# Expert weights carried in the exchanged rows, the gates' exponential by a power on GpSimd, and another order of drain and first loads: a gated cross-attention and mixture-of-experts block in float32 on one core

## The chip, the cores and the metric

The kernel runs on one core of a Trainium2 chip; the other cores are idle. The time is the device time of one execution in microseconds (us), and lower is better. All data and all arithmetic are float32 (indices are int32). Five engines work from queues of their own, each strictly in the order in which its instructions were written: TensorE (PE, with its weight loads PEld), VectorE (DVE), ScalarE (ACT), GpSimd (POOL) and SyncE (SP, which here only issues DMA transfers). They wait for one another by semaphores.

## The reference, cut to what matters

32 sequences of 128 tokens with 128 features, so 4096 tokens; 16 attention heads of 8 features; 8 routed experts (each token uses the best two) and 2 shared experts, all with 512 hidden units.

```python
x = x + tanh(g_xattn) * attention(layernorm(x), ctx, ctx, mask)      # 16 heads, softmax over 128 keys
xf = layernorm(x)
shared = mean over 2 experts of  gelu(xf @ sW1 + sb1) @ sW2 + sb2
gates = xf @ rW + rb                                                 # 8 gates per token
topk_vals, topk_idx = top_k(gates, 2)
topk_probs = softmax(topk_vals)
w = sum(topk_probs[..., None] * onehot(topk_idx))                    # two nonzero weights per token
h = gelu(xf @ W1[e] + b1[e]);  y[e] = h @ W2[e] + b2[e]
moe = sum over e of w[:, e] * y[e]
out = x + tanh(g_ffn) * (shared + moe)
```

## The kernel before, in words

**Stages.** The 32 sequences form 8 blocks of 4 (`BB`). A hand-written software pipeline runs over 32 steps (one sequence each) and 4 more that drain it; a step is two half-steps, numbered `where` = 0 to 7 within a block, and in each half-step `chores` inserts pieces of other work at the places `part` = -1, 0, 1, 2. These pieces are Python generators that are advanced one `yield` at a time: `before` (the next block's projections), `normed`, `after` (a finished block's second normalisation, gates, top two, and the slots of its rows), `sent` (the rows' scatter), and the filler `shared` (the two shared experts for a block). Since each queue runs in the order written, these insertions are the schedule.

**The filler.** `shared(i)` gives 8 pieces "h" (one matmul of 128x512 into a PSUM tile `ph`, L657, and its gelu on ACT, L661), then for each of 4 sequences a piece "y" (8 matmuls into `py`, L669) and a piece "a" (DVE adds `py` to the result rows `acc`, L676). `fill(kind)` advances it by one piece if the next one is of that kind, `more(n)` by n pieces. `ph`, `py`, and the small PSUM tiles `pu`, `pt_f`, `pgt`, `pr` share two PSUM buffers ("misc"), so each new one waits until the last but one has been read. The hidden values `h` have one buffer in the pool `ffn`.

**Gating and exchange.** `after` (L525 on) scales the rows into `xf[0]` on POOL (L315, L317), transposes them (`pt_f`) and multiplies by the gate weights (`pgt`, L548). DVE finds the best two by comparing all pairs (L554 to L579); POOL copies and advances the running counts (`front`, `seen`, L583 and L584). A step of its own (L587 to L601) takes exp on ACT and leaves both weights of each token, times tanh(g_ffn), in `wk2`. The next step ranks the rows by two small matmuls (`pr`, L604 and L607) and gives the slots `to_i` (L622). A row has 132 numbers (`ROW`): 128 features, the row's destination as an integer in column 128, and three unused columns. `sent` copies a sequence's rows to `xf[1]` and scatters both copies with an indirect DMA each (L634) to the DRAM buffer `xs`, which is sorted by expert.

**Schedule of the tiles.** After the last block `schedule` computes on DVE, from the counts (`pn`, L701), which expert and rows each of 39 tiles (32 of 256 rows, 7 of 128) gets: `ps_i` (L707), `table` (L756, L782), and the tiles' first-layer biases `b1t` (L786 to L795, 15 operations). Its scratch tile `space` lies in the pool `blk`. Then the attention's pools are closed, the pool `rt` is opened in their space, and the rest of filler blocks 4 and 5 is written ahead of the routed tiles. On SP, `padded` writes padding rows (L802) and `routed` loads, for each tile, two weight matrices (L814, L815), a bias row spread over the partitions (`b2t`, L818) and the rows (`xt`, L830). The first five tiles' weights are all issued ahead of their rows (L834, L835); afterwards the loads run five tiles ahead.

**Routed tiles.** Per tile PE transposes the rows (`pt_r`), does the first layer (`phr`, L855, gelu on ACT) and, one tile later, the second (`pyr`, L869). DVE adds `b2t` (L874), and POOL scatters each half of the result to its destination in the DRAM buffer `yd` (L879). Buffers: six for the weights and `b2t`, seven for `xt`, four for `y`.

**Tail.** After the last tile SP fetches `yd` by blocks (`y2`, L911), while PE does the filler of blocks 6 and 7. `combine` adds, for each of 4 sequences and 2 choices, `wk2` times the row (L920, eight operations of 128x128 a block), and `store` writes the rows out (L926).

Of the kernel before, what the change touches and what calls it, by code (L numbers as in the profile page):

```python
# [15 lines left out]
P = 128  # L16
BB = 4
# [16 lines left out]
def flamingo_kernel(  # L34
# [151 lines left out]
    nc.gpsimd.memset(mhalf, -0.5)  # L186
    ones = const.tile([P, P], F32, name="ones")
# [106 lines left out]
    wk2 = wts.tile([P, n_blocks * BB, 2], F32, name="wk2")  # L294
# [229 lines left out]
    def after(i, st):  # L524
# [55 lines left out]

        front = small.tile([P, BB, E], F32, tag="front", name=f"front_{i}")
        for b in range(BB):
            nc.gpsimd.tensor_copy(front[:, b, :], seen)  # L583
            nc.gpsimd.tensor_tensor(seen, seen, both[:, b, :], ALU.add)  # L584
        yield

        nc.scalar.activation(ge, ge, AF.Exp)  # L587
        gk = small.tile([P, 2, BB, E], F32, tag="gk", name=f"gk_{i}", bufs=1)
        nc.vector.tensor_tensor(
            gk, hot, ge.unsqueeze(1).to_broadcast([P, 2, BB, E]), ALU.mult  # L590
        )
        wk = small.tile([P, 2, BB], F32, tag="wk", name=f"wk_{i}")
        nc.vector.tensor_reduce(wk, gk, AX.X, ALU.add)
        ws = small.tile([P, BB], F32, tag="ws", name=f"ws_{i}")
        nc.vector.tensor_tensor(ws, wk[:, 0], wk[:, 1], ALU.add)
        nc.vector.reciprocal(ws, ws)
        nc.vector.tensor_scalar(ws, ws, tg[:, 1:2], None, ALU.mult)
        for k in range(2):
            nc.vector.tensor_tensor(
                wk2[:, i * BB : (i + 1) * BB, k], wk[:, k], ws, ALU.mult  # L600
            )  # L601
# [21 lines left out]
        st.update(xf=xf, to_i=to_i)  # L623
        yield
# [23 lines left out]


    def shared(i, two):  # L650
        h = ffn.tile([P, NS * NC, NB], F32, tag="h", name=f"h_{i}", bufs=1)
        for u in range(NS * NC // 2):
            ph2 = two(f"ph_{i}_{u}")
            for n in range(2):
                k, c = divmod(2 * u + n, NC)
                ph = ph2[n]
                nc.tensor.matmul(  # L657
                    ph, lhsT=W1_sb[:, k, c * P : (c + 1) * P], rhs=xfT_all[:, i, :],
                    start=True, stop=True,
                )  # L660
                nc.scalar.activation(  # L661
                    h[:, k * NC + c, :], ph, AF.Gelu,
                    bias=sb1c[:, k * NC + c : k * NC + c + 1],
                )
                yield "h"
        for b in range(BB):
            py = misc(f"py_{i}_{b}")[:, :P]
            for kc in range(NS * NC):
                nc.tensor.matmul(  # L669
                    py, lhsT=h[:, kc, b * P : (b + 1) * P],  # L670
                    rhs=W2_sb[:, kc // NC, kc % NC, :],
                    start=(kc == 0), stop=(kc == NS * NC - 1),
                )
            yield "y"
            a = acc[:, i * BB + b, :]
            nc.vector.tensor_tensor(a, py, a, ALU.add)  # L676
            yield "a"


    def schedule(ps_i, table, b1t):  # L680

        space = blk.tile([P, 2, BB, 2, P], F32, tag="kh", name="space").rearrange(
            "p s b j k -> p (s b j k)"
        )
        used = 0

        def temp(shape):
            nonlocal used
            size = math.prod(shape[1:])
            o = space[:, used : used + size]  # L690
            used += size
# [93 lines left out]
        part = temp([P, n_tiles, NC])  # L785
        for e in range(E):  # L786
            o = b1t if e == 0 else part
            nc.vector.tensor_tensor(
                o, mine[:, :, e : e + 1].to_broadcast([P, n_tiles, NC]),
                b1c[:, e, :].unsqueeze(1).to_broadcast([P, n_tiles, NC]), ALU.mult,  # L790
            )
            if e:
                nc.vector.tensor_tensor(b1t, b1t, part, ALU.add)
            if e % 3 == 2:
                yield  # L795
# [40 lines left out]
    def routed(table, b1t):  # L836
        weights = [load_weights(t, table) for t in order[:DEEP]]
        loaded = {t: (*w, load_rows(t, table)) for t, w in zip(order, weights)}

# [23 lines left out]
        def second(t, h):  # L863
# [3 lines left out]
            for n in range(parts(t)):  # L867
# [7 lines left out]
                y[:, : parts(t)], py, b2t.unsqueeze(1).to_broadcast([P, parts(t), P]), ALU.add  # L875
            )
# [39 lines left out]
    def combine(i, y2):  # L916
        for b in range(BB):
            for k in range(2):
                a = acc[:, i * BB + b, :]
                nc.vector.scalar_tensor_tensor(  # L920
                    a, y2[:, k, b, :], wk2[:, i * BB + b, k : k + 1], a, ALU.mult, ALU.add
                )
# [48 lines left out]
    with tc.manual_schedule(  # L971
# [12 lines left out]
        def chores(i, b, odd, part):  # L984
# [12 lines left out]
            elif part == 1:  # L997
                if where == 2:
                    step(behind)
                    fill("h") or fills("y")  # L1000
                elif where in (0, 6):
                    fills("y")
# [34 lines left out]
            elif where == 6:  # L1037
# [3 lines left out]
                step(behind)  # L1041
# [9 lines left out]
        def drain(where, part):  # L1051
# [3 lines left out]
            if part == 1:  # L1055
                if where > 2:
                    more(1)
                return
            if where == 0:
                step(behind)  # L1060
                ready.append(n_blocks - 2)
                step(sending)
                fills("y", "a")
            elif where == 1:
                step(behind)
                step(behind)
                step(sending)
                fills("y", "a")
# [5 lines left out]
            elif where == 3:  # L1074
                step(behind)
# [67 lines left out]
        more(2)  # L1143
        step(sending)
        for n in (3, 0, 3, 2, 1, 2):
            step(behind)
            more(n)
        sending = sent(last)
        ready.append(n_blocks - 1)
# [3 lines left out]
        steps = schedule(ps_i, table, b1t)  # L1153
        while step(steps):
# [5 lines left out]
        rt = ctx.enter_context(tc.tile_pool(name="rt", bufs=2))  # L1160
# [66 lines left out]
```

## Time and profile before

| what | value |
|---|---|
| median of 3 runs | 569.68 us (567.11 to 570.94) |
| the profiled execution | 571.77 us, of which the span of its instructions is 570.0 us |
| mean granted TensorE clock | 0.958 |
| DVE, ACT, POOL busy | 52%, 47%, 49% of the span |
| DMA moved | 53.82 MB, mean 94 GB/s |

The page of a profile lists busy time by engine, slices of the span with the TensorE clock that was granted (1.00 is full speed), the chain of work that ended last, and groups of instructions with what ended the idle time before them. Stretches of the span can be asked for one by one. By the start of their first instruction the stages are: preparation to about 20 us, the attention pipeline to 297 us, its drain with the last gating and the tile schedule to about 394 us, the routed tiles to 533 us, and the tail.

### The profile page before, as it was taken

What the parts mean: (1) busy time and instruction counts of PE and PEld (TensorE: products, weight loads), DVE (VectorE), ACT (ScalarE), POOL (GpSimd) and SP (SyncE); (2) the same over time, 40 slices, a digit from 0 to 9 for tenths busy, and PEclk for the clock granted to TensorE, in tenths of its full rate; (3) what the DMA queues carried; (4) which work ended last, traced back from release to release, by engine and by line L of the source; (5) the groups of instructions that cost most, each with busy time, mean ns of one, the idle gap of its engine ahead of it and who ended that gap; (6) DMA issues with size and microseconds to landing.
All of it is one profiled execution on the core that took longest, in us unless ns stands there. A gap on an engine that the chain in (4) does not pass through costs nothing.

```text
span 570.0 us, 11053 instructions
## 1 busy us (share of the span) xinstructions
PE 499.4 (88%) x3740; PEld 347.2 (61%) x3740; DVE 298.3 (52%) x961; ACT 266.8 (47%) x483; POOL 280.5 (49%) x559
## 2 busy tenths in 40 slices
PE   0586999989899898998989799788999999999977
PEld 0243545455565554546655377457999998888655
DVE  5445777596866877768782223821122221222186
ACT  1232757657644477565443533422445444444512
POOL 9541316158476585763836734600456455445400
PEclk9967999989999999999995799979999999999999
DMA  6410201002012010000000100365578788787293
GB/s 189 146 55 1 56 2 57 1 1 80 15 34 63 2 37 20 11 31 1 25 16 16 38 16 11 115 153 156 154 205 238 228 242 230 222 233 203 71 295 106
DMA packets 67719, 53.82 MB, mean 94 GB/s; under 512 B 6104, under 2 KB 59184, under 8 KB 67664
## 3 DMA queue, kind: packets, MB, share of 16 engines
q1 hardware_dynamic: 62016, 42.59, 27.3%
q0 software_dynamic: 5072, 10.26, 5.3%
q8 instruction: 30, 0.49, 0.3%
q10 hardware_dynamic: 576, 0.26, 0.2%
q14 instruction: 25, 0.20, 0.1%
HBM read 39.84 MB, written 13.25 MB: 93 GB/s over the span
## 4 chain that ended last, share of the span: by engine, by line
PE 62%; DVE 19%; DMA 6%; POOL 4%; ACT 3%; issue 3%; SPq 3%; POOLq 0%; DVEq 0%; ACTq 0%
PE pyr L869 10%; PE phr L855 9%; PE sc L414 8%; PE ph L657 7%; PE py L669 6%; DVE mexp L431 6%; PE num L472 4%; PE pk L374 3%; DMA xt<-xs 2%; PE pu L487 2%; DMA b2t<-in_L_ffn_b_dram 2%; DVE kT L377 2%; PE sw L414 2%; PE pq L358 2%; PE pgt L548 1%
## 5 line engine op out<-in xcount | busy, mean ns | idle before, releaser
L879 POOL DMA_INDIRECT yd<-y,xt x71 | 67.9, 957 | 94.3 <-DVE y L874 48.8
L431 DVE TENSOR_REDUCE mexp<-sc 128x4 f32<-128x512 f32 x128 | 82.2, 685 | 40.8 <-PE sw L414 34.2
L858 ACT ACTIVATE hr<-phr,b1t 128x256 f32<-128x256 f32 (+1 forms) x156 | 64.5, 454 | 79.1 <-PE phr L855 70.5
L464 ACT ACTIVATE pT<-sw 128x1024 f32<-128x1024 f32 x64 | 65.7, 1026 | 65.6 <-PE sw L414 65.6
L414 PE MATMUL sc<-kh,qT 32*128 32x256 f32 x512 | 77.4, 416 | 10.3 <-DVE mexp L431 10.1
L414 PE MATMUL sw<-qm,kT 32*128 32x256 f32 x512 | 76.7, 417 | 0.0
L657 PE MATMUL ph<-xfT_all,W_sb 128*128 128x512 f32 x128 | 67.1, 644 | 6.6 <-ACT h L661 2.4
L634 POOL DMA_INDIRECT xs<-xf,to_i x64 | 64.2, 1003 | 16.6 <-issue 6.7
L661 ACT ACTIVATE h<-ph,cols 128x512 f32<-128x512 f32 x64 | 43.9, 687 | 60.6 <-PE ph L657 60.4
L414 PEld LDWEIGHTS sc<-kh,qT 32*128 32x128 f32 x512 | 48.7, 192 | 35.8 <-issue 20.2
L869 PE MATMUL pyr<-w,hr 128*128 128x128 f32 x568 | 69.6, 275 | 0.0
L855 PE MATMUL phr<-xT,w 128*128 128x256 f32 (+1 forms) x312 | 68.1, 361 | 1.6 <-DVE xT L846 1.1
L669 PE MATMUL py<-W_sb,h 128*128 128x128 f32 x512 | 63.0, 283 | 6.0 <-DVE acc L676 6.0
L669 PEld LDWEIGHTS py<-W_sb,h 128*128 128x128 f32 x512 | 61.3, 199 | 10.4 <-DVE acc L676 6.3
L869 PEld LDWEIGHTS pyr<-w,hr 128*128 128x128 f32 x568 | 66.4, 192 | 0.5
L855 PEld LDWEIGHTS phr<-xT,w 128*128 128x128 f32 x312 | 53.0, 191 | 7.0 <-DVE xT L846 1.3
L381 POOL TENSOR_SCALAR kh<-kT,half 128x512 f32<-128x512 f32 x32 | 22.4, 714 | 61.3 <-DVE kT L377 61.3
L414 PEld LDWEIGHTS sw<-qm,kT 32*128 32x128 f32 x512 | 46.9, 192 | 0.9 <-issue 0.4
L846 DVE COPY xT<-pt_r 128x256 f32<-128x256 f32 (+1 forms) x39 | 15.6, 401 | 59.3 <-PE pt_r L844 58.8
L472 PE MATMUL num<-pT,v 128*32 128x256 f32 x512 | 42.9, 408 | 2.1 <-DVE qm L450 2.1
L657 PEld LDWEIGHTS ph<-xfT_all,W_sb 128*128 128x128 f32 x128 | 21.0, 198 | 35.3 <-ACT h L661 20.2
L874 DVE TENSOR_TENSOR y<-pyr,b2t 128x256 f32<-128x256 f32 (+1 forms) x39 | 15.6, 401 | 48.7 <-PE pyr L869 45.9
(210 smaller groups left out, 713.9 us busy)
## 6 DMA issues: line engine op xcount, KB each, us to landing
w<-in_L_ffn_W_dram SPq DMA_DIRECT2D x78, 256.0 KB, 3.2
xt<-xs SPq DMA_DIRECT2D x32, 132.0 KB, 4.1
y<-yd SPq DMA_DIRECT2D x16, 256.0 KB, 5.3
b2t<-in_L_ffn_b_dram SPq DMA_DIRECT2D x39, 64.0 KB, 8.3
x<-in_x_dram SPq DMA_DIRECT2D x8, 256.0 KB, 2.6
c<-in_ctx_dram SPq DMA_DIRECT2D x8, 256.0 KB, 4.2
mf<-md SPq DMA_DIRECT2D x7, 256.0 KB, 4.9
out_dram<-acc SPq DMA_DIRECT2D x7, 256.0 KB, 4.1
```

What stands on the lines that cost most here:

```text
L414: nc.tensor.matmul(out[:, r, s * 256 : s * 256 + 256], lhsT=lhsT[rr, s, :], rhs=rhs[rr, s, :, :].rearrange("p j n -> p (j n)"), start=True ...
L431: nc.vector.tensor_reduce(m[:, r], a["sc"][:, r, :].rearrange("p (s j k) -> p s j k", s=2, j=2), AX.X, ALU.max,)
L464: nc.scalar.activation(a["pT"][:, 2 * n : 2 * n + 2, :], a["sw"], AF.Exp)
L472: nc.tensor.matmul(num[32 * r : 32 * r + 32, :], lhsT=v[:, b, r, s, :], rhs=a["pT"][:, r, s * 256 : s * 256 + 256], start=True, stop=True,)
L634: ins = nc.gpsimd.indirect_dma_start(out=xs[:, :], out_offset=bass.IndirectOffsetOnAxis(ap=to_i[:, k, b : b + 1], axis=0), in_=xf[k][:, b, :],
L657: nc.tensor.matmul(ph, lhsT=W1_sb[:, k, c * P : (c + 1) * P], rhs=xfT_all[:, i, :], start=True, stop=True,)
L661: nc.scalar.activation(h[:, k * NC + c, :], ph, AF.Gelu, bias=sb1c[:, k * NC + c : k * NC + c + 1],)
L669: nc.tensor.matmul(py, lhsT=h[:, kc, b * P : (b + 1) * P], rhs=W2_sb[:, kc // NC, kc % NC, :], start=(kc == 0), stop=(kc == NS * NC - 1),)
L855: nc.tensor.matmul(ph, lhsT=w1[:, c * P : (c + 1) * P], rhs=xT, start=True, stop=True)
L858: nc.scalar.activation(h[:, c, :size], ph, AF.Gelu, bias=b1t[:, t, c : c + 1])
L869: nc.tensor.matmul(py[:, n, :], lhsT=h[:, c, n * P : (n + 1) * P], rhs=w2[:, c, :], start=(c == 0), stop=(c == NC - 1),)
L879: ins = nc.gpsimd.indirect_dma_start(out=yd[:, :], out_offset=bass.IndirectOffsetOnAxis(ap=xt.bitcast(I32)[:, n, P : P + 1], axis=0), in_= ...
```

## The change

Rows carry their weight: column 129 of `xf[k]` receives the weight of choice k, so the scatter brings it to the tile and the tile multiplies its result by it; `wk2` is gone and `combine` becomes two additions of 128x512 a block. The weights come from one number e2 = e^(second best gate - best gate): POOL computes it as a power of a constant, and DVE makes w0 = tanh(g_ffn) / (1 + e2) and w1 = w0 * e2 in the last step of `after`, behind `to_i`. The step with exp on ACT is gone, so `after` has one step fewer.

The order: in the last block's half-steps 0 and 2 no "y" piece is inserted any more; these two pieces come in the drain's half-steps 0 and 1. A "h" piece is added in the drain's half-step 2, and after the drain the filler is cut into smaller portions between the steps of the last gating, with `pr` behind the first instead of the fourth `py` of a filler block. `schedule` keeps its scratch values in the attention's two value tiles `v16` (which stay allocated), computes `b1t` in 8 larger operations, and yields more often. The first routed loads become: weights of tiles 0 and 1, rows of 0 and 1, then weights and rows tile by tile. The last block's `h` has a buffer of its own in `rt`.

```diff
+    euler = const.tile([P, BB], F32, name="euler")
+    nc.gpsimd.memset(euler, math.e)
...
-    wk2 = wts.tile([P, n_blocks * BB, 2], F32, name="wk2")
...
         nc.vector.tensor_tensor(both, hot[:, 0], hot[:, 1], ALU.add)
 
+        nc.vector.tensor_tensor(ge, ge, hot[:, 1], ALU.mult)
+        e2 = small.tile([P, BB], F32, tag="e2", name=f"e2_{i}")
+        nc.vector.tensor_reduce(e2, ge, AX.X, ALU.add)
+
         front = small.tile([P, BB, E], F32, tag="front", name=f"front_{i}")
         for b in range(BB):
             nc.gpsimd.tensor_copy(front[:, b, :], seen)
             nc.gpsimd.tensor_tensor(seen, seen, both[:, b, :], ALU.add)
-        yield
-
-        nc.scalar.activation(ge, ge, AF.Exp)
...
-        nc.vector.reciprocal(ws, ws)
-        nc.vector.tensor_scalar(ws, ws, tg[:, 1:2], None, ALU.mult)
-        for k in range(2):
-            nc.vector.tensor_tensor(
-                wk2[:, i * BB : (i + 1) * BB, k], wk[:, k], ws, ALU.mult
-            )
+        nc.gpsimd.tensor_tensor(e2, euler, e2, ALU.pow)
         yield
...
         st.update(xf=xf, to_i=to_i)
+
+        w = small.tile([P, BB], F32, tag="ws", name=f"ws_{i}")
+        nc.vector.tensor_scalar(w, e2, 1.0, None, ALU.add)
+        nc.vector.reciprocal(w, w)
+        nc.vector.tensor_scalar(xf[0][:, :, P + 1], w, tg[:, 1:2], None, ALU.mult)
+        nc.vector.tensor_tensor(xf[1][:, :, P + 1], xf[0][:, :, P + 1], e2, ALU.mult)
         yield
...
-        h = ffn.tile([P, NS * NC, NB], F32, tag="h", name=f"h_{i}", bufs=1)
+        pool = rt_pool if i == n_blocks - 1 else ffn
+        h = pool.tile([P, NS * NC, NB], F32, tag="h", name=f"h_{i}", bufs=1)
...
-        space = blk.tile([P, 2, BB, 2, P], F32, tag="kh", name="space").rearrange(
-            "p s b j k -> p (s b j k)"
-        )
+        spaces = [v.rearrange("p n c -> p (n c)") for v in v16]
...
-        part = temp([P, n_tiles, NC])
-        for e in range(E):
-            o = b1t if e == 0 else part
+        for c in range(NC):
             nc.vector.tensor_tensor(
-                o, mine[:, :, e : e + 1].to_broadcast([P, n_tiles, NC]),
-                b1c[:, e, :].unsqueeze(1).to_broadcast([P, n_tiles, NC]), ALU.mult,
-            )
-            if e:
-                nc.vector.tensor_tensor(b1t, b1t, part, ALU.add)
-            if e % 3 == 2:
-                yield
+                hop, mine,
+                b1c[:, :, c].unsqueeze(1).to_broadcast([P, n_tiles, E]), ALU.mult,
+            )
+            nc.vector.tensor_reduce(b1t[:, :, c], hop, AX.X, ALU.add)
+            yield
...
-        weights = [load_weights(t, table) for t in order[:DEEP]]
+        weights = [load_weights(t, table) for t in order[:2]]
         loaded = {t: (*w, load_rows(t, table)) for t, w in zip(order, weights)}
+        for t in order[2:DEEP]:
+            w = load_weights(t, table)
+            loaded[t] = (*w, load_rows(t, table))
...
+            nc.vector.tensor_tensor(
+                y[:, : parts(t)], y[:, : parts(t)],
+                xt[:, : parts(t), P + 1 : P + 2].to_broadcast([P, parts(t), P]), ALU.mult,
             )
...
-        for b in range(BB):
-            for k in range(2):
-                a = acc[:, i * BB + b, :]
-                nc.vector.scalar_tensor_tensor(
-                    a, y2[:, k, b, :], wk2[:, i * BB + b, k : k + 1], a, ALU.mult, ALU.add
-                )
+        a = acc[:, i * BB : (i + 1) * BB, :]
+        for k in range(2):
+            nc.vector.tensor_tensor(a, a, y2[:, k], ALU.add)
...
                 if where == 2:
                     step(behind)
-                    fill("h") or fills("y")
+                    i < n_blocks - 1 and (fill("h") or fills("y"))
                 elif where in (0, 6):
-                    fills("y")
+                    if where or i < n_blocks - 1:
+                        fills("y")
...
             if part == 1:
-                if where > 2:
+                fills("a")
+                if where < 2:
+                    fills("y")
+                else:
                     more(1)
                 return
...
         last = sts[n_blocks - 1]
-        more(2)
-        step(sending)
-        for n in (3, 0, 3, 2, 1, 2):
-            step(behind)
-            more(n)
-        sending = sent(last)
-        ready.append(n_blocks - 1)
...
+        more(3)
+        step(sending)
+        step(behind)
+        more(1)
+        step(behind)
+        step(behind)
+        more(2)
+        step(behind)
+        more(1)
+        step(behind)
+        sending = sent(last)
+        ready.append(n_blocks - 1)
+        more(1)
```

More of the change, by code (lines that the diff above doesn't have):

```diff
@@ L584, in after @@
             nc.gpsimd.tensor_tensor(seen, seen, both[:, b, :], ALU.add)
-        yield
[L587 to L590, printed above, removed]
-        )
[L592 to L595, printed above, removed]
-        nc.vector.reciprocal(ws, ws)
-        nc.vector.tensor_scalar(ws, ws, tg[:, 1:2], None, ALU.mult)
-        for k in range(2):
-            nc.vector.tensor_tensor(
-                wk2[:, i * BB : (i + 1) * BB, k], wk[:, k], ws, ALU.mult
-            )
+        nc.gpsimd.tensor_tensor(e2, euler, e2, ALU.pow)
         yield
@@ L647, in apart @@
         tc.add_to_no_dep_group(group, ins)
+    rt_pool = None
     def shared(i, two):
-        h = ffn.tile([P, NS * NC, NB], F32, tag="h", name=f"h_{i}", bufs=1)
+        pool = rt_pool if i == n_blocks - 1 else ffn
+        h = pool.tile([P, NS * NC, NB], F32, tag="h", name=f"h_{i}", bufs=1)
         for u in range(NS * NC // 2):
@@ L680, in schedule @@
     def schedule(ps_i, table, b1t):
-        space = blk.tile([P, 2, BB, 2, P], F32, tag="kh", name="space").rearrange(
-            "p s b j k -> p (s b j k)"
-        )
-        used = 0
+        spaces = [v.rearrange("p n c -> p (n c)") for v in v16]
+        used = [0, 0]
         def temp(shape):
-            nonlocal used
             size = math.prod(shape[1:])
-            o = space[:, used : used + size]
-            used += size
+            k = 0 if used[0] + size <= spaces[0].shape[1] else 1
+            o = spaces[k][:, used[k] : used[k] + size]
+            used[k] += size
+            assert used[k] <= spaces[k].shape[1]
             if len(shape) == 2:
@@ L1059, in drain @@
             if where == 0:
+                fills("a")
                 step(behind)
@@ L1062, in drain @@
                 step(sending)
-                fills("y", "a")
             elif where == 1:
+                fills("a")
                 step(behind)
@@ L1067, in drain @@
                 step(sending)
-                fills("y", "a")
             elif where == 2:
@@ L1074, in drain @@
             elif where == 3:
-                step(behind)
                 step(behind)
@@ L1142, in flamingo_kernel @@
         last = sts[n_blocks - 1]
-        more(2)
-        step(sending)
-        for n in (3, 0, 3, 2, 1, 2):
-            step(behind)
-            more(n)
-        sending = sent(last)
-        ready.append(n_blocks - 1)
         ps_i = const.tile([P, E], I32, name="ps_i")
@@ L1159, in flamingo_kernel @@
         first_part.close()
-        rt = ctx.enter_context(tc.tile_pool(name="rt", bufs=2))
+        rt = rt_pool = ctx.enter_context(tc.tile_pool(name="rt", bufs=2))
         ps_r = ctx.enter_context(tc.tile_pool(name="ps_r", bufs=4, space=PS))
```

## The prediction

> **What bounds the kernel now.** I read the slices first, then the chain of waits, then stretches of the span, and last the orders on each engine where PE pauses.
>
> ```profile
> PE 499.4 (88%) x3740; PEld 347.2 (61%) x3740; DVE 298.3 (52%) x961; ACT 266.8 (47%) x483; POOL 280.5 (49%) x559
> ...
> PEclk9967999989999999999995799979999999999999
> ...
> PE 62%; DVE 19%; DMA 6%; POOL 4%; ACT 3%; issue 3%; SPq 3%; POOLq 0%; DVEq 0%; ACTq 0%
> ```
>
> PE is the bound (88% busy, 62% of the chain), so time is lost where it pauses, and where its clock is below 1.00: the dips behind the start are at 299 to 328 and 370 to 385 us, the drain. The stretches (each column: busy us, count; then the clock):
>
> ```profile
> 285.00:345.00 60.00, 53.81 (x318) 31.07 (x318) 23.26 (x96) 25.44 (x42) 32.42 (x70) 0.83 0.07 22
> 345.00:380.00 35.00, 29.07 (x165) 22.21 (x165) 20.32 (x77) 10.24 (x14) 13.88 (x30) 0.90 0.27 79
> 397.00:478.00 81.00, 80.44 (x576) 75.27 (x575) 18.61 (x46) 39.23 (x95) 42.60 (x81) 1.00 0.74 210
> 478.00:531.00 53.00, 49.50 (x350) 45.52 (x349) 11.52 (x29) 24.31 (x60) 26.56 (x53) 1.00 0.75 208
> 531.00:570.00 39.00, 32.63 (x183) 21.62 (x181) 22.51 (x74) 11.33 (x18) 4.81 (x9) 0.99 0.60 170
> ```
>
> From 285 to 380 PE idles 6.2 + 5.9 = 12.1 us; five-us stretches give the clock 0.50, 0.50, 0.66 from 300 to 315, 0.53 and 0.79 from 320 to 330, 0.65 and 0.67 from 370 to 380; busy time times what the clock lacks makes 6.7 + 2.8 + 2.3 = 11.8 us. So 24 us can be won in the drain, and little in the routed tiles. The pauses:
>
> ```profile
> 299.53 0.89 PE L472 MATMUL num<-pT,v 128*32 128x256 f32 x8 [1.11 <-DVE qm L450]
> 321.14 2.07 PE L657 MATMUL ph<-xfT_all,W_sb 128*128 128x512 f32 x2 [2.31 <-DVE slot L611]
> 359.21 5.79 PE L657 MATMUL ph<-xfT_all,W_sb 128*128 128x512 f32 x12 [1.14 <-ACT h L661]
> 373.26 6.22 PE L669 MATMUL py<-W_sb,h 128*128 128x128 f32 x32 [4.50 <-DVE acc L676]
> 547.93 2.05 PE L669 MATMUL py<-W_sb,h 128*128 128x128 f32 x16 [1.46 <-DVE acc L676]
> ```
>
> Each names who held a PSUM buffer. The 32 matmuls at 373.26 take 6.22 us where 32 at 330.29 took 3.73: a pause costs again as a slow clock behind it. On DVE and ACT behind two of them:
>
> ```profile
> 319.22 0.23 DVE L589 TENSOR_TENSOR gk<-hot,ge 128x64 f32<-128x64 f32 x1 [3.12 <-ACT ge L587]
> ```
>
> ```profile
> 317.66 1.28 ACT L587 ACT_TABLE_LOAD   x1
> ...
> 319.20 1.28 ACT L661 ACT_TABLE_LOAD   x1
> ```
>
> exp between gelus costs two table loads, `gk` waits for it, and `slot` (which frees the buffer of `pr`) stands behind `gk`.
>
> **The change, part by part.** PE does the same matmuls between 285 us and the first routed tile (394.1 us); only their order changes. So the routed start moves by the change in lost time, if the rows are there. Replayed with the durations of this execution:
>
> (1) The pause of 1.11 us before `num` is filled: a `py` of 1.88 us (277.92 to 279.88 is such a one) now stands there, and the second moved `py` follows 4 us on. With the pause goes the half clock of 300 to 313.5: -1.1 - 6.7. The `pm` wait of 0.46 at 296.66 goes as well, since DVE's softmax step (0.84 waiting for exp, 1.3 of operations) stood ahead of it. New: `pt_f` waits for POOL's scaled rows, about +0.5. Sum -7.8.
>
> (2) Between 313 and 321 PE idles 3.5 us (0.78, 0.41, 2.31) and runs slowly for 2.8 us' worth. The exp is gone. But one table load to gelu stays, now ahead of a copy of `num` (0.8), and the two misc buffers still make `pr` and the `ph` behind it wait for one gelu each (0.9 + 0.9); half of such pauses may bring the slow clock (1.5). 4.1 for 6.3: -2.2.
>
> (3) The last gating loses something. `pr` now stands behind one `py`, not four. From the end of `pgt` it needs DVE 346.03 to 347.40 (1.4), POOL's `tie` (0.75), DVE from `ahead` to `both` (1.4) and eight POOL operations (352.02 to 353.82, 1.8); POOL's queue, with a scatter pair (2.75) and the `acc` addition (1.29) ahead of `tie`, adds 1.2: 6.8 with two hand-overs. PE has two `ph` (0.96) and a `py` (1.85) meanwhile. New pause 3.0, and slow clock behind it as at 373, 2.5: +5.5. What it buys: `pr` at about 344 instead of 355.4.
>
> (4) `b1t`: 15 operations (367.67 to 373.01) kept DVE from `acc`, which held `py`: 4.50 idle and 2.3 of clock. Now 4 pairs of 128x320 (0.49 each as L750 and L775) make 4.0 us, and beside them stand `ph`, which need no DVE. Only the third `py` waits, about 0.9: -5.9. If the `ph` were not there, 4 us would come back.
>
> (5) The 1.14 at 359.21 is the reload of gelu at 357.18 behind the last exp: -1.1.
>
> The drain: -7.8 - 2.2 + 5.5 - 5.9 - 1.1 = -11.5. Bounds: +0 if every new pause is as dear as the old (12 + 12), -17 if no clock is lost; I take the replay, which lies by the rows of (1) and (4).
>
> The rows are there in time: everything behind `pr` comes some 11 us sooner, but waits once for each of two `py`, so table and last scatter are done at about 358. The first weights used to wait for `b1t` in memory that the tiles share (2.8 us on SP); the scratch is elsewhere now. Two weight sets (2.25 us each on SP) precede the first rows: issued at 365, landed by 373 even at the longest landing on the page (8.3), and PE comes at 383. So the order of first loads wins nothing: the filler covers it. Without the cover the old order would cost 11 us of SP queue.
>
> Attention: per block seven DVE operations (1.3) leave half-step 6 and four of 0.2 enter half-step 7 ahead of `qm`; `ge` times `hot` and its reduction add 0.4 in half-step 4. At 122.27 DVE waited 0.23 for PE behind the softmax, so its removal gains 0 to 0.2; at 126.02 `qm` waited 0.18, so the new four delay it by 0.6, of which PE sees perhaps a fifth: +0.5 for five blocks (-1 to +3). POOL's power (1.03, as L315) lies in its idle (61.3 us before `kh`). Preparation: one memset, +0.1.
>
> Routed tiles: the multiplication (0.43 as L874's addition; 39 of them, 16 us) lies on DVE, 23% busy here. It delays each scatter by 0.43. SP's loads are nearly as slow as PE:
>
> ```profile
> 440.36 0.33 SPq L814 DMA_DIRECT2D w<-in_L_ffn_W_dram  x1
> 440.94 0.38 SPq L815 DMA_DIRECT2D w<-in_L_ffn_W_dram  x1
> 441.56 0.33 SPq L818 DMA_DIRECT2D b2t<-in_L_ffn_b_dram  x1
> 442.72 0.33 SPq L830 DMA_DIRECT2D xt<-xs  x1
> 443.83 0.33 SPq L814 DMA_DIRECT2D w<-in_L_ffn_W_dram  x1
> ```
>
> 3.47 us a tile at least, PE 3.55 on average; from 414.64 to 521.90 SP took 3.70, and that is where the 3.5 us of idle behind 478 come from. `xt` may only be reloaded when its scatter has landed; here that is over by 2.4 us (440.3, against 442.72), only tiles 1 and 2 wait. +0.5.
>
> Does it collide with POOL? At 136.56 a DVE operation with two SBUF inputs (`ge`) took 1.70 in place of 0.19, until POOL's `acc` addition (136.92, 1.28) was done; but at 366.75 L776, of the same kind, took its 0.19 during a scatter issue (366.10, 1.07). [...]
>
> Tail: DVE adds 2 x 0.7 a block (128x512; 0.49 at 320 columns plus a slope of 1.04 ns, 0.74 for L377 as upper bound) in place of 8 x 0.35, so `acc` frees `py` earlier: of the pauses 1.46, 0.74 and 0.84 some 0.7 remains, `y2` arriving 0.45 later included; the last also because `h` has its own buffer. -2.3. Behind it PE stays the end.
>
> Sum: -11.5 + 0.5 + 0.1 + 0.5 - 2.3 = -12.7. The profiled execution took 571.77 (span 570.0), 2.1 above the median 569.68; against the median: **557.0 us**.
>
> **The rivals.**
>
> 1. The drain gives back what it gains: `pr`'s pause 5 instead of 3 (POOL's scatters ahead of `tie`), the clock low through most of 300 to 345 again. For it: at 300 to 313 the clock stayed at 0.50 though PE never paused. Against: dense filler now stands there. -5: 565.
>
> 2. The clock stays full. My replay charges 4 us for slow clock after new pauses ((2) and (3)). The trace has 1.15 of idle at 358 without a dip, but one at 299.9 after 0.46 + 1.11. [...] -17: 552.
>
> 3. Slower: the routed tiles become bound by the scatter. Place: SP's `xt` load behind a scatter made later by the multiplication. It decides once the delay passes the 2.4 us of margin; 0.5 us a tile beyond it, over 33 loads, is +16, sum +3: 573. Against: delay 0.43, and POOL idles 1.43 before most scatters.
>
> 4. The change does nothing there: rows late, PE starved at the first tile for the 11 us won: 569.
>
> **How the numbers follow.** Forecast (551 to 561.5) 0.50; rival 1 (561.5 to 569) 0.24; rival 2 (546 to 551) 0.15; rival 3 0.08; rival 4 0.03. The range 549 to 567 leaves out rivals 3 and 4 and the ends of 1 and 2, about 0.18. One per cent is 5.7 us, about what a measurement can tell from no change: faster means below 564.0. Forecast, rival 2 and ten of rival 1's 24 make 0.75; slower, above 575.4, half of rival 3, 0.04; the same 0.21.
>
> **What would show it.** (1) the clock at 0.9 or more from 293 to 308, no pause over 0.6 before `num`. (2) one table load in the drain, no wait for `slot`. (3) a PE pause of 2 to 4 us before `pr`, slow matmuls behind it. (4) no pause over 1.5 behind `acc`. The first `pt_r` at about 383 instead of 394. Routed tiles 139 us long as before; three loads of `xt` at most waiting for scatters. Wrong, if `pt_r` waits for `xt` at its first tile, if the attention is over 3 us longer, or if the pause before `pr` is 5.

## The result, and the profile after it

| | before | changed |
|---|---|---|
| median, runs taken in turn on one chip | 568.46 us (567.11 to 570.94) | 553.30 us (552.36 to 555.38) |
| profiled execution, its span | 571.77, 570.0 | 555.38, 553.7 |
| start to the last `pv` | 268.4 | 269.1 |
| last `pv` to the first `pt_r` (the drain) | 125.7 | 109.6 |
| first `pt_r` to the first `ph` of filler block 6 (routed tiles) | 139.2 | 140.9 |
| from there to the end (tail) | 36.7 | 34.1 |

The changed kernel is faster: ratio 0.9733, 95% interval 0.9685 to 0.9782, or 15.2 us. The four stretches are read from the starts of the last `pv`, of the first `pt_r` and of the first of the last 32 `ph` (those of filler blocks 6 and 7); they sum to the spans, and the drain holds 16.1 of the 16.3 us by which the spans differ.

The page of the changed kernel, in the lines that were shown of before:

```profile
PE 488.4 (88%) x3740; PEld 340.4 (61%) x3740; DVE 302.4 (55%) x937; ACT 260.6 (47%) x471; POOL 289.7 (52%) x568
...
PEclk9975999999999999899999999999999999999999
...
PE 56%; DVE 20%; DMA 7%; issue 5%; SPq 4%; POOL 4%; ACT 3%; DVEq 0%; POOLq 0%; ACTq 0%
```

PE has the same 3740 matmuls and is busy 11 us less, since fewer run at the half clock. The row of the granted clock has no dip left in the drain; the single 8 in it is a half clock from 226.9 to 230.3 in the attention, as before had one from 118.9 to 122.3. The stretches of the span (busy us and count of PE, PEld, DVE, ACT and POOL; clock; DMA share; GB/s):

```profile
285.00:345.00 60.00, 55.87 (x397) 37.29 (x390) 26.84 (x118) 23.03 (x38) 41.33 (x90) 1.00 0.07 23
345.00:380.00 35.00, 32.41 (x183) 21.59 (x181) 16.03 (x48) 11.00 (x16) 8.34 (x14) 1.00 0.59 170
397.00:478.00 81.00, 78.23 (x555) 72.37 (x554) 27.42 (x68) 37.52 (x91) 43.17 (x83) 1.00 0.78 219
478.00:531.00 53.00, 51.20 (x343) 43.36 (x342) 16.24 (x41) 23.75 (x54) 25.74 (x49) 1.00 0.65 183
531.00:553.70 22.70, 18.59 (x112) 12.97 (x110) 11.12 (x21) 5.50 (x8) 0.00 (x0) 1.00 0.81 222
```

From 285 to 345 PE did 397 matmuls at a clock of 1.00, where before did 318 at 0.83. The whole drain, from the last `pv` to the first `pt_r`, in the same columns, first before and then changed:

```profile
268.44:394.14 125.70, 113.52 (x740) 74.28 (x738) 56.41 (x215) 48.33 (x76) 59.86 (x123) 0.89 0.20 59
269.15:378.68 109.53, 102.24 (x740) 67.86 (x738) 56.03 (x209) 42.34 (x69) 62.99 (x126) 1.00 0.24 70
```

The same 740 matmuls keep PE busy 11.3 us less, since none runs at the half clock any more, and PE idles 7.3 us instead of 12.2. So about 70% of the drain's gain is clock, the rest pauses. What is left of its pauses in the drain and in the tail:

```profile
339.51 0.41 PE L593 MATMUL pr<-both,upper 128*128 128x32 f32 x2 [0.58 <-DVE both L580]
341.19 0.41 PE L596 MATMUL pr<-front,ones 128*128 128x32 f32 x2 [1.27 <-POOL front L588]
341.43 2.03 PE L667 MATMUL py<-W_sb,h 128*128 128x128 f32 x16
...
348.80 6.84 PE L655 MATMUL ph<-xfT_all,W_sb 128*128 128x512 f32 x14 [0.68 <-DVE acc L674]
360.18 3.84 PE L667 MATMUL py<-W_sb,h 128*128 128x128 f32 x32 [0.97 <-DVE acc L674]
...
536.34 6.84 PE L655 MATMUL ph<-xfT_all,W_sb 128*128 128x512 f32 x14 [0.62 <-DVE acc L674]
```

The pause at `pr` is new and takes 1.85 us in two parts; the 4.50 at `acc` has become 0.68 and 0.97, the tail's three pauses one of 0.62. ACT has one table load in the drain where it had five:

```profile
307.71 1.28 ACT L659 ACT_TABLE_LOAD   x1
```

SyncE's loads go on at the pace they had, 3.46 us from one tile's weights to the next:

```profile
402.61 0.33 SPq L807 DMA_DIRECT2D w<-in_L_ffn_W_dram  x1
403.19 0.38 SPq L808 DMA_DIRECT2D w<-in_L_ffn_W_dram  x1
403.81 0.33 SPq L811 DMA_DIRECT2D b2t<-in_L_ffn_b_dram  x1
404.97 0.33 SPq L823 DMA_DIRECT2D xt<-xs  x1
406.07 0.33 SPq L807 DMA_DIRECT2D w<-in_L_ffn_W_dram  x1
```

### The profile page after: what moved, and what is told of

Its sections match the earlier page's. It is cut to its first block, busy times and chain, and to the rows that moved or that the text cites. A ratio compares the mean times of both kernels' runs of the same rounds, so it can differ in the third digit from the quotient of the medians.

```text
span 553.7 us, 11045 instructions
## 1 busy us (share of the span) xinstructions
PE 488.4 (88%) x3740; PEld 340.4 (61%) x3740; DVE 302.4 (55%) x937; ACT 260.6 (47%) x471; POOL 289.7 (52%) x568
## 4 chain that ended last, share of the span: by engine, by line
PE 56%; DVE 20%; DMA 7%; issue 5%; SPq 4%; POOL 4%; ACT 3%; DVEq 0%; POOLq 0%; ACTq 0%
PE pyr L865 8%; PE sc L415 8%; PE phr L851 7%; PE py L667 7%; PE ph L655 6%; DVE mexp L432 5%; PE num L473 4%; DMA xt<-xs 3%; PE pk L375 3%; PE pu L488 2%; DVE kT L378 2%; PE px L518 2%; PE pq L359 1%; PE pgt L549 1%; ACT qh L362 1%
## 5 line engine op out<-in xcount | busy, mean ns | idle before, releaser
L415 PE MATMUL sc<-kh,qT 32*128 32x256 f32 x512 | 78.2, 420 | 10.8 <-DVE mexp L432 10.7
L655 PE MATMUL ph<-xfT_all,W_sb 128*128 128x512 f32 x128 | 63.5, 616 | 1.9 <-DVE acc L674 1.3
L667 PE MATMUL py<-W_sb,h 128*128 128x128 f32 x512 | 61.3, 277 | 1.6 <-DVE acc L674 1.4
L667 PEld LDWEIGHTS py<-W_sb,h 128*128 128x128 f32 x512 | 59.0, 192 | 5.8 <-ACT h L659 3.7
L473 PE MATMUL num<-pT,v 128*32 128x256 f32 x512 | 41.3, 394 | 2.5 <-DVE qm L451 2.1
```

The source lines that it names most:

```text
L415: nc.tensor.matmul(out[:, r, s * 256 : s * 256 + 256], lhsT=lhsT[rr, s, :], rhs=rhs[rr, s, :, :].rearrange("p j n -> p (j n)"), start=True ...
L473: nc.tensor.matmul(num[32 * r : 32 * r + 32, :], lhsT=v[:, b, r, s, :], rhs=a["pT"][:, r, s * 256 : s * 256 + 256], start=True, stop=True,)
L655: nc.tensor.matmul(ph, lhsT=W1_sb[:, k, c * P : (c + 1) * P], rhs=xfT_all[:, i, :], start=True, stop=True,)
L667: nc.tensor.matmul(py, lhsT=h[:, kc, b * P : (b + 1) * P], rhs=W2_sb[:, kc // NC, kc % NC, :], start=(kc == 0), stop=(kc == NS * NC - 1),)
```

## The experiments

Twelve runs were made in three sessions of four, each session on another chip (6, 4 and 8), and each run is compared with the kernel before on the same chip. In the second and third session every kernel was slower, before too (568.6, 576.8 and 578.5 us); whether that is the chip or the hour is not told apart. The changed kernel itself ran in the third session only (after_2). In the first, whose kernel before agrees with that of the result above (568.6 and 568.5), kernels are set against the result; in the second, against one another.

| session | kernel | median, us | ratio to before, 95% interval | drain, routed, tail in its profile |
|---|---|---|---|---|
| 1 | no_move | 562.16 | 0.987 (0.9805 to 0.9934) | 117.0, 138.7, 33.8 |
| 1 | before_two_y | 563.09 | 0.9903 (0.9878 to 0.9929) | 117.0, 140.1, 36.1 |
| 1 | exp_act | 554.62 | 0.9746 (0.9703 to 0.979) | 112.6, 139.5, 33.2 |
| 1 | b1t_old | 553.37 | 0.9722 (0.9688 to 0.9757) | 109.7, 138.4, 33.4 |
| 2 | loads_old | 564.84 | 0.9767 (0.9726 to 0.9808) | 117.3, 146.1, 34.0 |
| 2 | wk2_back | 569.19 | 0.9853 (0.9809 to 0.9896) | 115.8, 145.7, 36.2 |
| 2 | h_shared | 563.09 | 0.9765 (0.9731 to 0.9799) | 115.2, 142.2, 33.8 |
| 2 | pr_late | 563.44 | 0.9765 (0.9731 to 0.98) | 114.8, 143.5, 34.3 |
| 3 | after_2 | 572.10 | 0.9886 (0.9841 to 0.9931) | 120.4, 147.6, 34.2 |
| 3 | wk2_back_2 | 573.53 | 0.9915 (0.988 to 0.9949) | 121.3, 145.0, 36.7 |
| 3 | order_old | 573.12 | 0.9914 (0.9879 to 0.9948) | 120.8, 148.6, 34.3 |
| 3 | pr_early | 573.19 | 0.9917 (0.9887 to 0.9948) | 120.8, 148.5, 34.0 |

**no_move: the two `py` back in their old half-steps.**

```diff
-                    i < n_blocks - 1 and (fill("h") or fills("y"))
+                    fill("h") or fills("y")
                 elif where in (0, 6):
-                    if where or i < n_blocks - 1:
-                        fills("y")
+                    fills("y")
```

> The changed kernel, but the two y pieces stay in the last block's half-steps 0 and 2. Theory A (they fill a pause, and the pause brings a slow clock): the pause of about 1.1 us before num near 299 us is back, the granted clock falls to 0.5 for 10 us or more behind it, and the time is 6 to 8 us above the changed kernel (559 to 561). Theory B (PE does the same matmuls wherever they stand; the gain comes from the exp that left ACT and from the earlier gating): at most 1.5 us above it (553 to 555).

562.16 us, 8.9 above the changed kernel (7.8 by the ratios). PE in its drain, and the stretches from 305 to 315:

```profile
303.18 0.92 PE L473 MATMUL num<-pT,v 128*32 128x256 f32 x8 [1.02 <-ACT oT L510]
304.58 1.76 PE L327 MATMUL pt_f<-ident,xf 128*128 128x128 f32 x4 [0.48 <-POOL xf L318]
306.28 2.08 PE L415 MATMUL sw<-qm,kT 32*128 32x256 f32 x8
```

```profile
305.00:310.00 5.00, 5.00 (x22) 2.43 (x21) 0.29 (x1) 1.61 (x2) 4.44 (x11) 0.50 0.09 30
310.00:315.00 5.00, 5.00 (x26) 4.13 (x23) 2.39 (x12) 0.67 (x2) 1.46 (x3) 0.50 0.00 0
```

The pause of 1.02 ahead of `num` is back, and the clock falls to half right behind it (0.84 over 300 to 305, so from about 303.4), ahead of the 0.48 at `pt_f`: eight `sw` take 2.08 us where at 300.77, at full clock, they took 1.13. Theory A holds, theory B fell. In this profile's drain PE idles 7.5 us and is busy 109.5, against 7.3 and 102.2 as changed: the drain's loss is slow clock alone. (Another 3.4 us lie ahead of the drain, with a half clock from 119.1 to 132.7 that b1t_old has as well.) Of the drain's, one stretch of 3.41 us (351.19 to 354.60) lies behind `pr`, where the moved `py` have no part. That the pause makes the clock fall, and not the sparser matmuls around it, is argued: the run put both back together.

**before_two_y: only those two `py` moved, in the kernel before** (the same guards, and `fills("y")` in part 1 of the drain's half-steps 0 and 1; the additions of `acc` behind them move along).

> The kernel before with only the two y pieces moved into the drain's half-steps 0 and 1. Theory A: clock 0.95 or more from 293 to 310 us, and 5 to 8 us less than before (560 to 563). Theory B: no more than 1.5 us less (567 or above).

563.09 us, 5.5 below before. The clock is 1.00 and 0.99 in 265 to 315, and what the rest of the change removes is still there:

```profile
314.37 1.77 PE L657 MATMUL ph<-xfT_all,W_sb 128*128 128x512 f32 x2 [2.06 <-DVE slot L611]
...
365.30 5.47 PE L669 MATMUL py<-W_sb,h 128*128 128x128 f32 x32 [4.49 <-DVE acc L676]
```

So the two moved pieces alone give about a third of the 15.2 us; taken out of the whole change they cost half of it or a little more, since without them the clock dips in the reordered drain too, and in no_move's profile once more behind `pr`.

**exp_act: the softmax's power as an exp on ACT again.**

```diff
-        nc.gpsimd.tensor_tensor(e2, euler, e2, ALU.pow)
+        nc.scalar.activation(e2, e2, AF.Exp)
```

> The changed kernel, but e2 comes from exp on ACT and not from a power on GpSimd. Both drained blocks then cost two more table loads of 1.28 us each on ACT. Theory A (what held PE was slot standing behind gk on DVE; that order is gone, only ACT is busier by 2.6 us twice): 0.5 to 2.5 us above the changed kernel (554 to 556). Theory B (the exp on ACT is the main loss): 4 us or more above it (557 to 560).

554.62 us: 1.3 above the changed kernel, 0.7 by the ratios, with intervals that overlap. The table loads are back,

```profile
309.50 1.28 ACT L657 ACT_TABLE_LOAD   x1
...
311.76 1.28 ACT L588 ACT_TABLE_LOAD   x1
...
313.28 1.28 ACT L657 ACT_TABLE_LOAD   x1
```

and PE's pauses beside them are 0.78, 0.60 and 0.28 at 313.61 to 316.23. The 2.31 at `slot` does not come back, because nothing ahead of `slot` waits for the exp here: the weights are made behind `to_i`, from 317.03 on. `slot` waits for PE alone:

```profile
315.98 0.19 DVE L598 TENSOR_TENSOR slot<-pr,first_slot 128x32 f32<-128x32 f32 x1 [2.10 <-PE pr L594]
```

So this run prices an exp on ACT, not the old order with the weights ahead of `slot`, which no run put back alone. By size it lies in theory A's range, but no difference is shown.

**b1t_old: `b1t` by the old fifteen operations** (the loop over experts of before, in the new order of the drain).

> The changed kernel with the 15 old operations for b1t; order and scratch place stay. Theory A (what counts is that ph pieces, which need no DVE, stand beside them): acc comes about 1.2 us later, PE pauses 2.2 instead of 0.97 us before the third py near 360 us, 1 to 2 us above the changed kernel (554 to 555). Theory C (the 15 small operations themselves held PE): the pause of 4 us and more returns with a slow clock behind it, 5 to 7 us above (558 to 560).

553.37 us, ratio 0.9722: no difference from the changed kernel's 0.9733. PE's waits for `acc` are hardly longer:

```profile
352.16 6.84 PE L655 MATMUL ph<-xfT_all,W_sb 128*128 128x512 f32 x14 [0.67 <-DVE acc L674]
...
363.66 3.84 PE L667 MATMUL py<-W_sb,h 128*128 128x128 f32 x32 [1.08 <-DVE acc L674]
```

Theory C (that the fifteen operations bring back the 4.5 us) fell, and theory A's 1 to 2 us were not seen. What the operations stand beside decides, not their number; order_old below is the other half of that.

**loads_old: the first routed loads in the old order.**

```diff
-        weights = [load_weights(t, table) for t in order[:2]]
+        weights = [load_weights(t, table) for t in order[:DEEP]]
         loaded = {t: (*w, load_rows(t, table)) for t, w in zip(order, weights)}
-        for t in order[2:DEEP]:
-            w = load_weights(t, table)
-            loaded[t] = (*w, load_rows(t, table))
```

> The changed kernel with the first routed loads in the old order (all five tiles' weights, then five tiles' rows). Theory A (the prediction's, that this order is worth nothing here because filler covers it): the first rows are asked for some 12.4 us behind the first weights instead of 4.6, so at about 369 instead of 361, and would land by about 372, still ahead of the first pt_r at 378.7; the time stays at 553.4 us (552.5 to 554.5). Rival: the tensor engine needs the rows of the first tiles earlier than the trace makes it look, or the transfers of five weights crowd the rows: first pt_r 2 to 6 us later, 555 to 559.

Ratio 0.9767, beside 0.9765 and 0.9765 for h_shared and pr_late. The rows are asked for 11.3 us behind the first weights, and still 12.3 us ahead of the first `pt_r` (387.1). SyncE's issues:

```profile
363.50 0.37 SPq L807 DMA_DIRECT2D w<-in_L_ffn_W_dram  x1
...
374.76 4.85 SPq L823 DMA_DIRECT2D xt<-xs  x5
```

Nothing on PE waits for `xt` there. Theory A holds against the kernels of its session: the new order of loads is worth nothing that this shows.

**wk2_back and wk2_back_2: the weights in the combine again** (the same kernel twice; `wk2` kept in SBUF, no multiplication of the tile's rows).

```diff
-        a = acc[:, i * BB : (i + 1) * BB, :]
-        for k in range(2):
-            nc.vector.tensor_tensor(a, a, y2[:, k], ALU.add)
+        for b in range(BB):
+            for k in range(2):
+                a = acc[:, i * BB + b, :]
+                nc.vector.scalar_tensor_tensor(
+                    a, y2[:, k, b, :], wk2[:, i * BB + b, k : k + 1], a, ALU.mult, ALU.add
+                )
```

> The changed kernel with the experts' weights applied in the combine again (wk2 kept in SBUF, sixteen multiply-adds a block pair as before), without the 32 multiplications of a tile's rows; all else as changed. Theory A (the prediction's two terms): the tail gets its 2.3 to 2.5 us back, and the routed part loses what the multiplication of 0.425 us a tile put on it, 0.5 by the prediction and 1.7 at most by the traces: 554.2 to 555.4 us in all. Theory B: the multiplication costs the routed part nothing, its 1.7 us more being SyncE's order of issues: about 555.9. Theory C: it costs the routed part as much as the tail gains: 553.4. The trace tells them apart by the time from the first pt_r to the last block's ph (140.9 us as changed) and from there to the end (34.1).

> The weights in the combine again, a second time: its ratio was 0.0087 above those of three neighbours, some 5 us, where the tail's 2.1 us in its trace (36.2 against 33.8 to 34.3) accounts for half. Theory A: the tail is all and the rest was scatter between runs; 2 to 2.6 us above the changed kernel beside it. Theory B: the routed part gets longer too when the weights move to the combine, by the waits for xt (7.2 us in that trace, 2.7 in a neighbour's): 4.5 to 6 us above.

The first time it was 4.4 to 6.1 us above its neighbours, the second time 1.4 above the changed kernel (0.0029, or 1.7 us, by the ratios, intervals overlapping). The first excess lies above all three theories of its expectation, and what it had over the tail did not repeat; so theory B of the second expectation fell, and 1.4 to 1.7 is below theory A's 2 to 2.6, though within the intervals. The tail is the part that repeats: 36.2 and 36.7 against 33.8 to 34.3. The combine in wk2_back, and in the changed kernel:

```profile
L918 DVE SCALAR_TENSOR_TENSOR acc<-y,wk,acc 128x128 f32<-128x128 f32 x64 | 20.2, 349 | 9.1 <-DMA y<-yd 8.0
```

```profile
L919 DVE TENSOR_TENSOR acc<-acc,y 128x512 f32<-128x512 f32 x16 | 11.1, 693 | 10.8 <-DMA y<-yd 10.6
```

9.1 us less of DVE; in the tail that is 1.9 to 2.7 us of time. The routed part without the multiplication took 145.7 and 145.0, with it 142.2 to 148.6 in the same sessions: its price is below the scatter.

**h_shared: the last block's `h` in the common buffer again.**

```diff
-        pool = rt_pool if i == n_blocks - 1 else ffn
+        pool = ffn
```

> The changed kernel with the last block's h in the same buffer as the others again. Theory A (the prediction's step 5): its first gelu waits for the previous block's last py, and the tensor engine for the gelu: a wait of about 1.1 us comes back near 349 to 360, 554.2 to 554.6 us. Rival: the order of the drain now leaves other pieces between the two, or the wait lies inside one that is there anyway (0.68 and 0.97 behind acc): no change, 553.4.

Ratio 0.9765, no difference from loads_old and pr_late; PE waits for no gelu there, and the tail's one pause is 0.67 at `acc` as in its neighbours. The rival held: the buffer is worth nothing here. (The expectation named step 5; the prediction itself had put the buffer in the tail.)

**pr_late: `pr` behind two `py`.**

```diff
-        more(1)
+        more(2)
         step(behind)
         sending = sent(last)
         ready.append(n_blocks - 1)
-        more(1)
```

> The changed kernel with pr behind two of the last py groups instead of one. Theory A: the two pauses at pr (0.58 and 1.27, 1.85 us together) are covered by the 3.84 us of the second py, and nothing takes their place, since the chain from pr to the first pt_r has 10 us to spare: 551.5 to 552.0 us. Rival: pieces that would have stood behind acc are used up ahead of pr, so the waits for acc (0.68 and 0.97) grow, or the rows arrive late: 553 to 554.5.

Ratio 0.9765, as its neighbours that keep the pause. The pause is gone in the trace:

```profile
346.50 0.41 PE L596 MATMUL pr<-front,ones 128*128 128x32 f32 x2 [0.30 <-POOL front L588]
```

The changed kernel itself was not in that session, and the expected 1.5 us is inside the intervals: whether it beats the changed kernel is open.

**after_2: the changed kernel again.**

> The changed kernel once more, so that the kernels beside it have it as a yardstick on the same chip: its ratio to before was 0.9733, interval 0.9685 to 0.9782. Both theories: 0.970 to 0.979.

572.10 against 578.48 us: ratio 0.9886, outside the expected range and outside the first interval. The gain here was 6.4 us where it had been 15.2. Of the 16.9 us between its profile and the first one, 10.8 lie in the drain and 6.7 in the routed tiles; attention and tail agree within 0.7. PE, and then ACT, in its drain:

```profile
345.32 0.41 PE L596 MATMUL pr<-front,ones 128*128 128x32 f32 x2 [1.27 <-POOL front L588]
345.56 3.34 PE L667 MATMUL py<-W_sb,h 128*128 128x128 f32 x16
...
356.77 2.08 PE L655 MATMUL ph<-xfT_all,W_sb 128*128 128x512 f32 x2 [2.90 <-issue]
```

```profile
358.61 1.39 ACT L659 ACTIVATE h<-ph,cols 128x512 f32<-128x512 f32 x2 [16.77 <-issue]
```

"Issue" is time in which the engine waited for nothing that the profile shows. In the first trace that gelu started at 348.22, as soon as its `ph` was there; here it starts at 358.61, and `ph` wait for its buffer. In the first trace a packet of an instruction queue (q14) lies between 348 and 352, here the next one behind `pr` of that queue between 356 and 360, though `pr` itself is only 4.1 us later. The two other sessions share this: PE's pauses from 268 us on that end with nothing that the profile shows sum to 2.9 to 9.3 us in each of the eight traces of sessions 2 and 3, and to 0.0 in the six of the result and of session 1. On PE the first trace has no such gap in 290 to 385; this one has gaps of 0.38, 1.68 and 2.90. What the engines waited for there is not shown: no run tried whether the packet that lies later is the cause. There is no trace of before in that session, so it is also open why it lost less than the changed kernel.

**order_old: the old sequence of pieces in the last gating.**

```diff
-        more(3)
-        step(sending)
-        step(behind)
-        more(1)
-        step(behind)
-        step(behind)
         more(2)
-        step(behind)
-        more(1)
-        step(behind)
+        step(sending)
+        for n in (3, 0, 3, 3, 2):
+            step(behind)
+            more(n)
```

> The changed kernel with the old sequence of pieces in the last gating (two, then 3, 0, 3, 3 and 2 behind its steps): pr stands behind four py and one ph, and of the last but one block's pieces none are left for the table's steps. Theory A (the prediction's steps 3 and 4 taken together): the 1.85 us of pauses at pr go, but the steps of the table and of b1t run beside py that wait for acc, 1.5 to 4.5 us and perhaps 2 of slow clock behind them, and rows come later: 1.5 to 5 us above the changed kernel beside it. Theory B: the new order wins nothing by itself, the pauses at acc were made by b1t's fifteen operations alone: the same or up to 1.9 us below.

573.12 us, 1.0 above after_2 (1.6 by the ratios), intervals overlapping. The trace shows the mechanism. PE and DVE:

```profile
368.22 5.46 PE L667 MATMUL py<-W_sb,h 128*128 128x128 f32 x32 [4.23 <-DVE acc L674]
```

```profile
367.48 0.49 DVE L787 TENSOR_REDUCE b1t<-v 128x40 f32<-128x320 f32 x1
367.88 0.28 DVE L674 TENSOR_TENSOR acc<-py,acc 128x128 f32<-128x128 f32 x1
```

With the new, short `b1t`, the wait for `acc` is back at 4.23, and a slow clock behind it (32 matmuls in 5.46 instead of 3.73), because `py` stand beside the table's operations again: DVE works on the table and `b1t` without a gap from 359.5 until that `acc` at 367.88. In exchange the pauses at `pr` are gone. Theory A's mechanism is shown; its net price is not separable from zero.

**pr_early: `pr` ahead of the `py` that covers it.**

```diff
-        more(1)
         step(behind)
         sending = sent(last)
         ready.append(n_blocks - 1)
-        more(1)
+        more(2)
```

> The changed kernel with pr ahead of the py that it stands behind, so that the tensor engine has 1.9 us less to do while VectorE and GpSimd make both and front. Theory A (a pause alone does not bring the slow clock when the work around it is dense): the pause grows from 1.85 to about 3.7 us, the clock stays at 1.00 in 335 to 350, 1.9 us above the changed kernel beside it. Theory B (the prediction's charge: about half a clock for some us behind such a pause): the granted clock falls below 0.8 behind it, 3.5 to 5 us above.

573.19 us, 1.1 above after_2 (1.8 by the ratios), intervals overlapping. The pause is 3.62 and the clock falls behind it:

```profile
342.45 0.60 PE L593 MATMUL pr<-both,upper 128*128 128x32 f32 x2 [2.64 <-DVE ge L582]
344.04 0.63 PE L596 MATMUL pr<-front,ones 128*128 128x32 f32 x2 [0.98 <-POOL front L588]
344.48 5.96 PE L667 MATMUL py<-W_sb,h 128*128 128x128 f32 x32
```

32 matmuls take 5.96 us, 2.2 more than at full clock. Theory B's dip is there; but after_2, its yardstick, has a dip at the same place with half the pause, which is why the time is only 1.1 to 1.8 us longer, where theory B had 3.5 to 5.

## Why the prediction was right, point by point

The forecast of 557.0 was 3.7 us above the measured 553.3, and the time lies in its interval of 551 to 561.5; the profiled spans fell by 16.3 where its sum was 12.7. Where the time would be won, in the drain, and by what, was foreseen; that the interval held has some luck in it. What the profile shows is rival 2, a drain at full clock. By the prediction's own terms that rival costs -12.7 - 4.0 = -16.7, so 553.0 us; the prediction wrote 552 and gave it the interval 546 to 551, so that the rival's time lies in the forecast's interval. (In the same way its bound of -17 for a drain without lost clock would be -11.5 - 4.0 = -15.5.)

- **Step (1), -7.8: held.** No pause over 0.6 ahead of `num` (0.38), the clock 1.00 from 285 to 345. (The `py` read as 1.88 us takes 2.03 at 277.92; nothing hangs on it.) Undone alone it costs 7.8 to 8.9 us, with the dip behind `pr` in its profile; done alone it gives 5.5. This is the largest single part, and what it removes is mostly slow clock behind a short pause.
- **Step (2), -2.2: too small.** The one table load and the small waits came as said, but 1.0 us of pauses were left in 306 to 324 (0.38, 0.28, 0.38) instead of 2.6, and none of the 1.5 of slow clock. The reading of the 2.31 (`slot` behind `gk`, `gk` behind the exp) agrees with exp_act, where an exp that nothing ahead of `slot` waits for does not bring it back; the old order itself was not put back.
- **Step (3), +5.5: mis-sized, the main error.** "New pause 3.0, and slow clock behind it as at 373, 2.5." The pause was 1.85 and this execution had no slow clock. The charge was not baseless, though: nine of the profiled executions have that same pause of 1.83 to 1.85 us, with sixteen matmuls of `py` behind it. These took 2.03 us, which is full clock, in three (the changed kernel, b1t_old, loads_old), and 2.57, 2.93, 3.28, 3.30, 3.34 and 3.54 in six. In each of the six the half clock lasts 3.41 us, with PE busy throughout, and so costs 1.7 us, not 2.5; 0.5 to 1.5 of it fall on those sixteen. What tells the three from the six is said behind this list.
- **Step (4), -5.9: size right, half of its reason wrong.** The waits for `acc` are 0.68 and 0.97 where 0.9 was said, without slow clock. The step named two causes: fewer operations for `b1t`, and `ph` beside them. The first is worth nothing (b1t_old); the second is the cause (order_old brings 4.23 back).
- **Step (5), -1.1: held in the trace** (no reload of gelu, no wait for it at 349 to 360), not separable in time; where exp_act brings the reload back, at 353.23, PE waits 0.34 for the gelu behind it.
- **The drain in sum:** 16.1 us won, 11.5 predicted. Split by kind, the steps had -7.8 for the clock and -3.7 for pauses; measured were -11.3 and -4.9. So 3.5 of the missing 4.6 is clock: the 4.0 of slow clock charged in (2) and (3) that this execution did not have, less 0.5 because before had lost 11.3 by it, not 11.8. The rest is pauses: 1.15 less than said at `pr`, 1.6 less in (2), 0.75 more at `acc`, and some 0.8 more in small ones elsewhere in the drain. The routed part and attention took 1.4 more than said, without which the total would lie further from the forecast.
- **First loads, 0: held** (loads_old). The first `pt_r` came at 378.7 instead of about 383, with no wait for `xt`.
- **Attention, +0.5:** 0.7. **Tail, -2.3:** 2.5, and 1.9 to 2.7 by wk2_back and wk2_back_2; all of it is the combine, the separate `h` adding nothing.
- **Routed tiles, +0.5:** 1.7 in this profile, six waits for `xt` of 4.6 us in all, against 3.5. But the stretch took 138.4 to 139.5 in three other executions of kernels with the multiplication in the first session, and 140.1 in one without it (before_two_y). The multiplication takes 425 ns (424 to 426) in each of the 32 large tiles, never stretched by GpSimd's scatters beside it. No run shows the 0.5 us a tile of rival 3's sum; the multiplication kept to its own 425 ns. So rival 3 did not come, and neither did rival 4.
- **Not foreseen: how far the gain depends on the session.** In the third session the changed kernel took 572.1 us, above the range of 549 to 567, beside 578.5 for before. The prediction was right for the chip and hour of the first runs; it held nothing on the pauses of the third.

In each of the fourteen traces all changes of the granted clock lie whole multiples of 3.41 us apart (in the trace of before, those at 299.79, 313.44, 320.27 and 327.09 us lie 4, 2 and 2 times 3.41 us apart), and where they lie differs from one execution to the next. Such a stretch of 3.41 us is called a window here. Cut at such places, the stretches around the pause at `pr` are, first in after_2 and then in the changed kernel's first profile (time, busy us of PE to POOL, clock):

```profile
342.63:346.04 3.41, 1.58 (x13) 1.28 (x12) 1.61 (x9) 0.00 (x0) 1.87 (x8) 1.00 0.00 0
346.04:349.45 3.41, 3.41 (x18) 3.41 (x18) 1.85 (x10) 0.00 (x0) 2.33 (x5) 0.50 0.05 17
```

```profile
339.55:342.97 3.42, 2.15 (x18) 2.04 (x19) 1.59 (x9) 0.00 (x0) 2.64 (x9) 1.00 0.00 0
342.97:346.38 3.41, 3.41 (x33) 3.41 (x32) 2.25 (x12) 0.00 (x0) 2.46 (x5) 1.00 0.13 41
```

In after_2 both parts of the pause fell into one window, which left PE busy 46% of it (1.58 of 3.41), and the next window ran at half clock. In the changed kernel the windows divided the pause, and PE was busy 63%. The other executions with this pause agree in the main: 46% in four more with a dip and 58% in the sixth, 53% in b1t_old and 74% and 72% in loads_old without one.

A window need not be idle for the half clock to follow it. Between 285 and 400 us the fourteen hold 18 windows at full clock in which PE was busy 46% or less, and the half clock followed each; of 12 windows from 49% to 59% it followed two, of 393 at 60% or more one. Elsewhere, from 60 us on, two windows of 43% and 45% had no dip behind them, so the boundary is not sharp, and no run moved a pause within a window on purpose.

## What to carry to other kernels

A pause of 1 to 2 us of the bounding engine can cost several times its length when the clock falls behind it (here 1.1 us of pause and 6.7 of slow clock, where four windows in a row stayed slow; 1.7 for a single one), so work that can be moved is worth most where the matmuls are sparse and already wait. Where an operation queue holds up a buffer, look first at what stands beside it: a shorter `b1t` won nothing here (ratio 0.9733, against 0.9722 in b1t_old), and other neighbours took a wait of 4.50 us to 0.68 and 0.97. Price a slow clock behind a new pause as a chance with a size, not as a certainty: by these traces it comes when a window of 3.41 us is left less than about half busy (behind 18 of 18 that were 46% busy or less in 285 to 400 us), and where the windows lie changes from one execution to the next. Repeat a gain of a few per cent in another session, on another chip, before counting on its size.

## What the runs showed of the hardware that was not expected

- The granted clock changes on a grid of 3.41 us whose place differs in each execution. Identical pauses of 1.85 us at `pr` were followed by full clock in three profiled executions and by one window at half clock in six, 1.7 us each; in five of the six, and in none of the three, the window ahead had PE busy less than half of it.
- The same kernel took 553.3 us in one session and 572.1 in another, before it 568.5 and 578.5. In the eight traces of sessions 2 and 3 engines wait, up to 2.9 us at a time on PE, for nothing that the profile shows, above all in the drain and the routed tiles; in the six others PE never does there. An instruction packet lies late beside one of these waits, between 356 and 360 us where the first trace has it between 348 and 352; that the one causes the other was not tried, and a difference between the chips was not separated from it.
